# Layer 0 of a two-layer scan network: the partitions onto which three shifted copies for the dilated taps are written

## The chip, the cores and the metric

The kernel runs on one core of a Trainium2 chip. The metric is the device time of one execution in microseconds. Before the change three runs took 26,064.51, 26,128.44 and 26,154.08 us; their median, 26,128.44 us, is the time that the change is compared with.

## The reference, cut to what matters

The input is `x` with shape (4, 128, 128, 192): four images of 128 x 128 points with 192 channels. Two layers follow each other. Layer 0 normalises, projects to 384 channels, runs a 3x3 depthwise convolution, then a scan over all 16,384 points of an image. The scan's result, `h_map`, goes through three depthwise 3x3 convolutions with dilations 1, 3 and 5, which are added. Only this last part is touched by the change:

```python
def _dwconv_replicate(x, w, dil, pad):
    xp = jnp.pad(x, ((0, 0), (0, 0), (pad, pad), (pad, pad)), mode='edge')
    return lax.conv_general_dilated(xp, w, (1, 1), 'VALID', rhs_dilation=(dil, dil),
        dimension_numbers=('NCHW', 'OIHW', 'NCHW'), feature_group_count=x.shape[1])
...
h1 = _dwconv_replicate(h_map, k3, 1, 1)
h2 = _dwconv_replicate(h_map, k3_1, 3, 3)
h3 = _dwconv_replicate(h_map, k3_2, 5, 5)
h_f = alpha[0] * h1 + alpha[1] * h2 + alpha[2] * h3
```

A layer norm over channels, a gate and an output projection follow. Layer 1 is a different network with four scans and isn't touched.

## The kernel before, in words

**Stages.** `transpose_in` brings the input to channel-major form (span 0 to about 480 us). `layer0` follows; its loads of shifted copies are issued from 561.3 to 5,767.7 us. `in_conv`, `scans` and `outputs` do layer 1 in the rest of the span.

**Layer 0.** An image is cut into 16 chunks of 8 image rows (1,024 points), and the 384 channels into 3 blocks of 128 partitions. For each chunk and block, `project_in` (TensorE, L431), `conv_in` (nine products on ScalarE, L488, added by GpSimd, L493) and `scan` (VectorE, L580) produce the scan's result `hp`, padded at the sides to rows of 138 elements, and `store` (L559) writes it to the DRAM scratch `hpad`. One chunk behind, `half` handles 4 image rows (512 points) at a time, and `item` (from L594) does one block of 128 channels of such a half: 4 images x 16 chunks x 2 halves x 3 blocks are 384 items.

**The dilated taps.** For each of the two dilations 5 and 3, an item loads three copies of its rows from `hpad`, shifted by -dilation, 0 and +dilation image rows. The tile `sa` has 96 partitions and 4 groups of 4 x 138 elements. The 128 channels of a block are seen as 4 groups of 32, so the free dimension counts the groups and the partitions hold 32 channels x 3 copies. `load` (L603 to L608) issues three DMAs from the SP queue, one a copy. Each writes 32 partitions, a row of 2,208 bytes for each of 4 groups, 276 KB in all. `mm` (L610 to L619) then runs 12 matmuls: for each of three horizontal offsets and four groups, the weights `diag[:, d, s, k, g]` (96 x 32) hold one tap weight for each channel and copy, so that one matmul sums three vertical taps of 32 channels into 32 partitions of the PSUM bank `o`. There are two dilations, so an item has 6 loads and 24 such matmuls. The eight taps of dilation 1 beside the middle one are done by VectorE (`taps`, L635) from a tile `hh` that is loaded by L624, and the middle tap is folded into `diag`.

**What sets the order.** `Order.emit` plans layer 0 on the host from costs written beside each step and replays the steps in that order on all engines. A load of shifted copies is one planned step with cost 1.5 and size 848e3, a matmul step of 12 costs 2.7, and the planner's DMA rate is 250e3 bytes a microsecond. Each of the tiles `sa0` and `sa1` has two buffers, and the PSUM bank has two. SP takes its DMAs in the planned order; before each it waits for the buffer to be free.

**Set up once.** `mask` (L318 to L320, 96 x 32) has a one where a partition belongs to a channel of the group; `diag` (L322 to L328) is the product of the tap weights `wk` with it. `wk` and `wc` are arranged on the host in `layout`.

Of the kernel before, what the change touches and what calls it, by code (L numbers as in the profile page):

```python
# [12 lines left out]
ALU = mybir.AluOpType  # L13
# [8 lines left out]
HC = C // 2  # L22
NB = 3
PAD = 5
HW_ = W + 2 * PAD
# [175 lines left out]
class Maker:  # L201
# [60 lines left out]
    def layer0(self, xT, x1T, hpad, xsd, gn_in, gnd, gn_out, w, ident, p96, eps):  # L262
# [6 lines left out]
        nc, tc = self.nc, self.tc  # L269
        ctx = ExitStack()  # L270
        with ctx:
# [16 lines left out]
            wk = cp.tile([HC, 2, 3, NB, 4], F32, name="wk")  # L288
            nc.sync.dma_start(wk, w["wk0"])
            wc = cp.tile([HC, 2, NB, 4], F32, name="wc")  # L290
# [10 lines left out]
            def v(k, i):  # L301
                return vec[:, k, i : i + 1]
# [13 lines left out]
                )  # L316
                nc.vector.tensor_tensor(wk[:, 0, 1], wk[:, 0, 1], wc[:, d], ALU.add)
            mask = cp.tile([HC, 32], F32, name="mask")  # L318
            nc.vector.tensor_tensor(mask, ident[:HC, 0:32], ident[:HC, 32:64], ALU.add)
            nc.vector.tensor_tensor(mask, mask, ident[:HC, 64:96], ALU.add)  # L320
            nw = 2 * 3 * NB * 4
            diag = cp.tile([HC, 2, 3, NB, 4, 32], F32, name="diag")  # L322
            nc.vector.tensor_tensor(
# [10 lines left out]
            def buf(tag, bufs, *shape, pool=p1, stream=None):  # L334
                return Buf(pool, tag, bufs, list(shape), stream)
# [258 lines left out]
            def item(b, j, h, k, Cb):  # L594
                r0 = PAD + R * j + 4 * h
                lo, hi = (r0 - 2 * PAD) // R, (r0 + 3) // R
                near = [("h", b, c, k) for c in range(max(lo, 0), min(hi, NCH - 1) + 1)]
                src = hpad[b][k * 128 : k * 128 + 128].rearrange("(g c) x -> c g x", c=32)
                o = buf("hf", 2, 128, 512, pool=psH)
                for d, dil in enumerate(DILS):  # L600
                    t = buf(f"sa{d}", 2, HC, 4, 4 * HW_)

                    def load(t=t, dil=dil):  # L603
                        for a in range(3):
                            c = (r0 + (a - 1) * dil) * HW_
                            nc.sync.dma_start(
                                t()[32 * a : 32 * a + 32], src[:, :, c : c + 4 * HW_]
                            )  # L608

                    def mm(t=t, d=d, dil=dil):  # L610
                        x = t().rearrange("p g (r w) -> p g r w", w=HW_)
                        for s in range(3):
                            c0 = PAD + (s - 1) * dil
                            for g in range(4):
                                nc.tensor.matmul(  # L615
                                    o()[32 * g : 32 * g + 32], diag[:, d, s, k, g],
                                    x[:, g, :, c0 : c0 + W],
                                    start=(d == 0 and s == 0), stop=(d == 1 and s == 2),
                                )  # L619

                    op("SP", 1.5, load, reads=near, writes=[t], size=848e3, early=-192)
                    op("PE", 2.7, mm, reads=[t], writes=[o], early=-456)
                hh, xr = buf("hh", 2, 128, 6, HW_), buf("xsr", 2, 128, 512)
                op("SP", 0.5, lambda: nc.sync.dma_start(  # L624
                    hh().rearrange("p r w -> p (r w)"),
                    hpad[b][k * 128 : k * 128 + 128, (r0 - 1) * HW_ : (r0 + 5) * HW_],
                ), reads=near, writes=[hh], size=424e3)
                c1 = j * T + h * 512
                op("SP", 0.4, lambda: nc.sync.dma_start(
                    xr(), xsd[b][k * 128 : k * 128 + 128, c1 : c1 + 512]  # L630
                ), reads=[("xs", b, j, k)], writes=[xr], size=262e3)
                def taps(which):
                    o3 = o().rearrange("p (r w) -> p r w", w=W)
                    for col, dy, dx in which:
                        nc.vector.scalar_tensor_tensor(  # L635
                            o3, hh()[:, 1 + dy : 5 + dy, PAD + dx : PAD + dx + W],
                            v(k, V0_K + col), o3, ALU.mult, ALU.add,
                        )

                for q in range(0, 8, 2):  # L640
                    op("DVE", 1.57, lambda q=q: taps(NEAR[q : q + 2]), reads=[hh], writes=[o], early=-966)
                y = buf("y", 6, 128, 512)

                def combine():
                    nc.vector.tensor_tensor(o(), o(), Cb(), ALU.mult)
                    nc.vector.scalar_tensor_tensor(  # L646
                        y(), xr(), v(k, V0_DS), o(), ALU.mult, ALU.add
                    )

                op("DVE", 1.45, combine, reads=[Cb, xr], writes=[o, y])  # L650
                return y
# [946 lines left out]
def pair_pack(w):  # L1598

    t = np.zeros((128, 6, 128), np.float32)  # L1600
    t[:, AA] = w[:128, :128]
    t[:64, MA] = w[128:, :128]
    t[64:, MC] = w[128:, :128]
    t[:, AM, :64] = w[:128, 128:]
    t[:, CM, 64:] = w[:128, 128:]
    t[:64, MM, :64] = w[128:, 128:]
    t[64:, MM, 64:] = w[128:, 128:]
    return t


def block_rows(v):

    return np.concatenate([v[:128], v[128:], v[128:]])


def layout(a):
    n = {k: np.asarray(v) for k, v in a.items()}
    l0 = {k[8:]: v for k, v in n.items() if k.startswith("L0_conv_")}
    l1 = {k[8:]: v for k, v in n.items() if k.startswith("L1_conv_")}
    w = {"x": n["x"].reshape(B, L, C)}  # L1620
    w["p96"] = np.kron(np.eye(HC // 6), np.full((6, 6), 1 / 6)).astype(np.float32)

    w["win0"] = l0["Win"].T
    xp = np.zeros((NB * 128, 32), np.float32)
    xp[:, : DR + 2] = l0["x_proj_w"].T
    w["xp0"] = xp
    dtw = np.zeros((2, 32, NB * 128), np.float32)
    dtw[:, :DR] = l0["dt_w"].T
    dtw = dtw.reshape(64, NB * 128)
    w["dtw0"] = dtw  # L1630
    w["wout0"] = l0["Wout"].T
    w["alpha"] = l0["alpha"].reshape(1, 3)
    w["vec0"] = np.concatenate(
        [l0["conv_w"].reshape(-1, 9)]
        + [l0[x].reshape(-1, 1) for x in ("conv_b", "dt_b", "A_logs", "Ds")]
        + [l0["k3"].reshape(-1, 9)]
        + [l0[x].reshape(-1, 1) for x in ("ln_g", "ln_b")],
        axis=1,
    )


    wk = np.stack([l0[x].reshape(NB, 4, 32, 3, 3) for x in ("k3_2", "k3_1")])
    wk = wk.transpose(4, 3, 0, 5, 1, 2).copy()
    wc = np.zeros((3, 32, 2, NB, 4), np.float32)
    for d, x in enumerate(("k3", "k3_1")):
        wc[1, :, d] = l0[x].reshape(NB, 4, 32, 9)[..., 4].transpose(2, 0, 1)
    wk[1, :, 1, 1] = 0
    w["wk0"], w["wc0"] = wk.reshape(HC, 2, 3, NB, 4), wc.reshape(HC, 2, NB, 4)

    w["wx1"] = pair_pack(l1["in_proj_w"][:, :C])  # L1650
    w["wz1"] = pair_pack(l1["in_proj_w"][:, C:])
    xp = np.zeros((128, 4, 3, 128), np.float32)
    dtw = np.zeros((128, 4, 3, 128), np.float32)
    nd = DR + 2 * NS
    for k in range(4):
        pw, dw = l1["x_proj_w"][k], l1["dt_w"][k]
        xp[:, k, 0, :nd] = pw[:128]
        xp[:64, k, 1, :nd] = pw[128:]
        xp[64:, k, 1, 64 : 64 + nd] = pw[128:]
        xp[:, k, 2, 64 : 64 + nd] = pw[:128]  # L1660
        dtw[:DR, k, 0] = dw[:, :128]
        dtw[:DR, k, 1, :64] = dw[:, 128:]
        dtw[64 : 64 + DR, k, 1, 64:] = dw[:, 128:]
        dtw[64 : 64 + DR, k, 2] = dw[:, :128]
    w["xp1"], w["dtw1"] = xp, dtw
    wo = np.zeros((128, 3, C), np.float32)
    wo[:, 0] = l1["out_w"][:128]
    wo[:64, 1] = l1["out_w"][128:]
    wo[64:, 2] = l1["out_w"][128:]
    w["wout1"] = wo  # L1670
    w["vec1"] = block_rows(
        np.concatenate(
            [l1["conv_w"].reshape(C, 9)]
            + [l1[x].reshape(C, 1) for x in ("conv_b", "ln_g", "ln_b")]
            + [l1["dt_b"].T],
            axis=1,
        )
    )

    w["al1"] = l1["A_logs"].reshape(4, 3, 64, 2, NS // 2).transpose(3, 2, 1, 0, 4).reshape(128, -1)  # L1680
    w["ds1"] = np.tile(l1["Ds"].reshape(4, 3, 64).transpose(2, 1, 0), (2, 1, 1))
    return {k: np.ascontiguousarray(v) for k, v in w.items()}
# [23 lines left out]
```

## Time and profile before

| What | From the page or the trace |
|---|---|
| Runs | 26,064.51 to 26,154.08 us, median 26,128.44 us |
| Profiled execution | span 26,077.3 us; what lies around the span isn't listed |
| TensorE busy | 23,595.6 us, 90% of the span |
| VectorE, ScalarE, GpSimd busy | 84%, 80%, 79% |
| DMA moved | 4,171.84 MB, mean 160 GB/s |
| `sa<-hpad` | 2,304 issues, 276 KB each, 8.0 us from issue to landing |
| L615, matmuls on `sa` | 18,432 instructions, 2,191.8 us busy |
| L635, the near taps | 3,072 instructions, 2,316.2 us busy |

The page cuts the span into 40 slices of about 652 us. Layer 0 fills the slices from the first to the ninth. "Busy" is time in which an instruction of the engine was under way; matmuls are pipelined, and their ends are modelled. The DMA digit is the mean busy share of 16 DMA engines.

### The profile page before, as it was taken

The page shows a single profiled execution, that of the slowest core. Times are in us where ns is not written, and L with a number is a line of the kernel's source. Part 1 is how long each engine was busy: PE and PEld are TensorE (multiplying, and loading weights), DVE is VectorE, ACT ScalarE, POOL GpSimd, SP SyncE. Part 2 cuts the span into 40 slices and gives each one's busy share as a digit, 9 for nine tenths or more (in the row PEclk, how much of TensorE's full clock was granted, in tenths as well). Part 3 has the DMA queues.
Part 4 walks back from the last instruction along what each step waited for, and adds up shares of the span by engine and source line. Part 5 has one row for each costly group of instructions (what it writes and reads, how often), then busy time and mean ns, then how long its engine had stood idle before and what let it go on. Part 6 is the DMA issues. An engine that isn't in the chain of part 4 may idle for free.

```text
span 26077.3 us, 435537 instructions
## 1 busy us (share of the span) xinstructions
PE 23595.6 (90%) x168196; PEld 8682.5 (33%) x168196; DVE 21939.2 (84%) x15401; ACT 20827.2 (80%) x24211; POOL 20540.0 (79%) x9962
## 2 busy tenths in 40 slices
PE   4999999998799999999999999999999999999699
PEld 2323232222233333333333333333333333333245
DVE  3889888888788889998988988888998989999643
ACT  5989899966688888888888888888888888888543
POOL 3999899955588888888888888888888888899500
PEclk6999999999899999999999999999999999999899
DMA  6999999985544444444444444444544444455563
GB/s 205 246 246 251 239 249 246 243 219 200 162 127 130 130 129 135 135 127 116 125 117 132 135 132 128 129 130 131 137 134 132 121 119 121 131 139 138 193 232 107
DMA packets 1646421, 4171.84 MB, mean 160 GB/s; under 512 B 236800, under 2 KB 387776, under 8 KB 1641280
## 3 DMA queue, kind: packets, MB, share of 16 engines
q1 hardware_dynamic: 1644352, 4143.97, 58.0%
q8 instruction: 1333, 21.84, 0.4%
q14 instruction: 736, 6.03, 0.1%
HBM read 3203.95 MB, written 939.10 MB: 159 GB/s over the span
## 4 chain that ended last, share of the span: by engine, by line
PE 47%; DVE 21%; ACT 13%; issue 7%; DMA 6%; POOL 5%; SPq 1%; DVEq 0%; POOLq 0%; ACTq 0%
DVE h L1250 14%; PE f L1217 13%; PE Y L1264 10%; ACT h L1228 6%; PE hf L615 5%; ACT dA L1244 3%; PE s L1071 3%; POOL hc L1256 2%; PE s L1094 2%; POOL xs L493 2%; PE g L706 2%; PE f L723 2%; DVE hf L635 2%; PE z L828 1%; DMA C<-cs 1%
## 5 line engine op out<-in xcount | busy, mean ns | idle before, releaser
L1256 POOL TENSOR_TENSOR hc<-h,C 128x1024 f32<-128x1024 f32 x6144 | 14345.2, 2364 | 2265.0 <-PE Y L1264 1087.3
L1250 DVE TENSOR_TENSOR_SCAN h<-dA,st,h 128x1024 f32<-128x1024 f32 x5760 | 13131.7, 2334 | 708.5 <-ACT st L1280 275.2
L1228 ACT COPY h<-f 128x1024 f32<-128x1024 f32 (+3 forms) x8192 | 6343.2, 801 | 2094.0 <-PE f L1217 2028.7
L1217 PE MATMUL f<-D,dT 32*64 32x256 f32 x98304 | 7087.0, 404 | 795.8 <-ACT h L1228 649.7
L1264 PE MATMUL Y<-hc,sel 128*64 128x512 f32 x24576 | 6928.0, 651 | 479.9 <-POOL hc L1256 223.6
L1244 ACT ACTIVATE dA<-d,alog 128x1024 f32<-128x1024 f32 x6144 | 6917.7, 1126 | 313.0 <-DVE h L1250 260.4
L1217 PEld LDWEIGHTS f<-D,dT 32*64 32x64 f32 x98304 | 3253.3, 136 | 6620.9 <-ACT h L1228 4804.6
L493 POOL TENSOR_TENSOR xs<-xs,pr 128x1024 f32<-128x1024 f32 x1536 | 3640.4, 2372 | 251.8 <-ACT pr L488 185.7
L635 DVE SCALAR_TENSOR_TENSOR hf<-hh,vec,hf 128x512 f32<-128x512 f32 x3072 | 2316.2, 754 | 251.4 <-PE hf L615 125.9
L1264 PEld LDWEIGHTS Y<-hc,sel 128*64 128x64 f32 x24576 | 1314.5, 140 | 2959.6 <-issue 1770.9
L615 PE MATMUL hf<-sa,diag 96*32 96x512 f32 x18432 | 2191.8, 614 | 78.5 <-DVE y L646 43.6
L1143 DVE TENSOR_TENSOR D<-s,mask 128x1024 f32<-128x1024 f32 x1024 | 1241.7, 1213 | 842.6 <-PE s L1137 842.6
L488 ACT ACTIVATE pr<-xi,vec 128x1024 f32<-128x1024 f32 x1536 | 1706.7, 1144 | 175.8 <-POOL xs L493 172.8
L615 PEld LDWEIGHTS hf<-sa,diag 96*32 96x32 f32 x18432 | 555.0, 111 | 1616.5 <-issue 1348.7
L1104 POOL TENSOR_TENSOR u<-l,u 128x1024 f32<-128x1024 f32 x384 | 908.2, 2365 | 165.2 <-ACT l L1097 137.1
L1250 DVE TENSOR_TENSOR_SCAN h<-dA,h 128x1024 f32<-128x1024 f32 x384 | 856.8, 2276 | 64.3 <-ACT dA L1244 32.2
L1094 PE MATMUL s<-pj,w 128*128 128x512 f32 x1536 | 894.2, 665 | 7.1 <-ACT l L1097 2.0
L1071 PE MATMUL s<-u,w 128*128 128x512 f32 x1536 | 749.2, 625 | 53.2 <-DMA prev<-xc 52.5
L706 PE MATMUL g<-xz,w 96*128 96x512 f32 x1536 | 769.1, 626 | 28.6 <-DVE y L699 14.8
L1097 ACT ACTIVATE l<-s,vec 128x512 f32<-128x512 f32 x768 | 529.1, 689 | 325.3 <-PE s L1094 320.7
L1137 PEld LDWEIGHTS s<-ident,pj 128*128 128x128 f32 x4096 | 550.0, 195 | 593.0 <-issue 251.6
L939 DVE SCALAR_TENSOR_TENSOR acc<-xi,vec,acc 128x1024 f32<-128x1024 f32 x384 | 715.0, 1862 | 26.8
(209 smaller groups left out, 21241.3 us busy)
## 6 DMA issues: line engine op xcount, KB each, us to landing
C<-cs SPq DMA_DIRECT2D x4096, 256.0 KB, 4.8
sa<-hpad SPq DMA_DIRECT2D x2304, 276.0 KB, 8.0
d<-delta SPq DMA_DIRECT2D x1536, 256.0 KB, 4.1
u<-xc SPq DMA_DIRECT2D x384, 512.0 KB, 4.7
delta<-l SPq DMA_DIRECT2D x384, 512.0 KB, 3.7
y<-y SPq DMA_DIRECT2D x1536, 128.0 KB, 3.3
hh<-hpad SPq DMA_DIRECT2D x384, 414.0 KB, 8.0
hpad<-hp SPq DMA_DIRECT2D x192, 552.0 KB, 8.3
```

Of the source, the lines that this page charges most:

```text
L488: op("ACT", 1.1, lambda pr=pr, t=t: nc.scalar.activation(rows(pr()), x()[:, t // 3 : t // 3 + R, t % 3 : t % 3 + W], AF.Copy, scale=v(k, V ...
L493: op("POOL", 2.38, lambda pr=pr: nc.gpsimd.tensor_tensor(o(), o(), pr(), ALU.add), reads=[pr], writes=[o], early=-390)
L615: nc.tensor.matmul(o()[32 * g : 32 * g + 32], diag[:, d, s, k, g], x[:, g, :, c0 : c0 + W], start=(d == 0 and s == 0), stop=(d == 1 and s ...
L635: nc.vector.scalar_tensor_tensor(o3, hh()[:, 1 + dy : 5 + dy, PAD + dx : PAD + dx + W], v(k, V0_K + col), o3, ALU.mult, ALU.add,)
L1071: nc.tensor.matmul(g(), wt()[:, 0, i], uu[i]()[:, 512 * c : 512 * c + 512], start=(i == 0), stop=(i == 2),)
L1094: op("PE", 0.9, lambda g=g, c=c: nc.tensor.matmul(g(), wt()[:, 1, i], x()[:, 512 * c : 512 * c + 512], start=True, stop=True,), reads=[wt, ...
L1217: nc.tensor.matmul(gs()[64 * jn : 64 * jn + 64, n, 256 * a : 256 * a + 256], td()[rt, r // 64, 2 * sb + a], tD()[rt, a, 256 * jn : 256 * j ...
L1228: nc.scalar.copy(H[:, at : at + nq, 256 * sb : 256 * sb + 256].rearrange("p q (a r s) -> p q a r s", a=2, s=32)[:, :, :, 2 * rp : 2 * rp + 2],
L1244: op("ACT", 1.16, lambda: nc.scalar.activation(a(), d(), AF.Exp, scale=alog[:, c : c + 1]), reads=[d], writes=[a], table="exp", early=-522)
L1250: nc.vector.tensor_tensor_scan(hs[:, way], a()[:, way], hs[:, way], 0.0 if at == 0 else s0()[:, q : q + 1], ALU.mult, ALU.add,)
L1256: op("POOL", 2.4, lambda: nc.gpsimd.tensor_tensor(t(), hs, tC(), ALU.mult), reads=[hq, tC], writes=[t])
L1264: nc.tensor.matmul(ym()[64 * th : 64 * th + 64], sel, t()[:, 512 * th : 512 * th + 512], start=(q == 0), stop=(q == NQ - 1),)
```

## The change

The partition of a channel `c` and a copy `a` in the tile `sa` becomes `3*c + a`; it was `32*a + c`. So a load writes every third of the 96 partitions, where it wrote 32 that lie side by side. Bytes, number of DMAs, number of matmuls and their shapes stay. The mask, and the tap weights that the host lays out, are rearranged to match: on the device one reduction takes the place of two additions, once in the kernel.

```diff
             mask = cp.tile([HC, 32], F32, name="mask")
-            nc.vector.tensor_tensor(mask, ident[:HC, 0:32], ident[:HC, 32:64], ALU.add)
-            nc.vector.tensor_tensor(mask, mask, ident[:HC, 64:96], ALU.add)
+            nc.vector.tensor_reduce(
+                mask, ident[:HC, :HC].rearrange("p (c a) -> p c a", a=3),
+                mybir.AxisListType.X, ALU.add,
+            )
...
                         for a in range(3):
                             c = (r0 + (a - 1) * dil) * HW_
-                            nc.sync.dma_start(
-                                t()[32 * a : 32 * a + 32], src[:, :, c : c + 4 * HW_]
-                            )
+                            nc.sync.dma_start(t()[a:HC:3], src[:, :, c : c + 4 * HW_])
...
-    wk = wk.transpose(4, 3, 0, 5, 1, 2).copy()
-    wc = np.zeros((3, 32, 2, NB, 4), np.float32)
+    wk = wk.transpose(3, 4, 0, 5, 1, 2).copy()
+    wc = np.zeros((32, 3, 2, NB, 4), np.float32)
     for d, x in enumerate(("k3", "k3_1")):
-        wc[1, :, d] = l0[x].reshape(NB, 4, 32, 9)[..., 4].transpose(2, 0, 1)
-    wk[1, :, 1, 1] = 0
+        wc[:, 1, d] = l0[x].reshape(NB, 4, 32, 9)[..., 4].transpose(2, 0, 1)
+    wk[:, 1, 1, 1] = 0
```

## The prediction

> **What bounds the kernel now.** The change touches layer 0 alone, so I asked first for the busy times before, in and after the stretch in which shifted copies are loaded and used (window view; the numbers after each stretch are its length and then busy us of TensorE, weight loads, VectorE, ScalarE, GpSimd, the granted clock, the DMA share and GB/s):
>
> ```profile
> core 0: us, PE busy (x) PEld busy (x) DVE busy (x) ACT busy (x) POOL busy (x), PEclk, DMA share, GB/s
> 0.00:560.00 560.00, 236.96 (x1218) 172.33 (x1218) 188.13 (x311) 254.40 (x269) 148.19 (x97) 0.69 0.65 203
> 560.00:5790.00 5230.00, 5056.38 (x26065) 1551.19 (x26064) 4576.00 (x5897) 4621.13 (x5120) 4642.89 (x2940) 0.97 0.96 244
> 5790.00:26077.00 20287.00, 18302.26 (x140918) 6959.00 (x140916) 17175.07 (x9194) 15951.67 (x18823) 15748.94 (x6927) 0.94 0.49 137
> ```
>
> In these 5,230 us two resources are nearly full: DMA at 0.96 and TensorE at 5,056 us (97%, with modelled ends). VectorE, ScalarE and GpSimd stand at 87 to 89%. Later the DMA share is 0.49, so nothing there can gain from cheaper transfers.
>
> Is the DMA slow because of these very loads? I looked for neighbouring stretches with and without them (DMA view of two 10 us stretches: the rate, then what was issued):
>
> ```profile
> DMA packets 1371, 3.35 MB, mean 335 GB/s; under 512 B 170, under 2 KB 362, under 8 KB 1369
> ...
> q1 hardware_dynamic: 1369, 3.32, 100.9%
> ```
>
> ```profile
> DMA packets 1120, 2.20 MB, mean 220 GB/s; under 512 B 124, under 2 KB 124, under 8 KB 1120
> ...
> q1 hardware_dynamic: 1120, 2.20, 105.2%
> ...
> sa<-hpad SPq DMA_DIRECT2D x6, 276.0 KB, 6.1
> ```
>
> The first is 4,550 to 4,560 us, when other transfers are moving; the second is 4,560 to 4,570, when all data packets are the 2,208-byte rows of `sa`. The engines are full in both, yet the rate is 335 against 220 GB/s. So a byte of `sa` costs half as much again as another. The packet records say the same: over layer 0 a 2,208-byte packet takes 166 ns in the median and 89 ns in the quickest tenth, two humps a factor of two apart, while packets of 2,048 bytes from other loads have a median of 89 ns.
>
> Does anyone wait for it? The waits of SP and the engines, and the chain that ended last (line, us in total, times, longest):
>
> ```profile
> SPq L606 <- PE hf L615: 699.2, 392, 8.8
> SPq L624 <- DVE hf L635: 520.0, 214, 12.3
> SPq L606 <- DMA sa<-hpad: 354.6, 439, 2.5
> ```
>
> ```profile
> 1803.06 9.72 DMA sa<-hpad
> ...
> 1812.86 9.86 DMA hpad<-hp
> ...
> 1822.73 10.46 DMA sa<-hpad
> ...
> 1833.28 11.77 DMA hpad<-hp
> ```
>
> SP waits mostly for engines to free the double buffers, so DMA isn't the pacer everywhere; but there are stretches such as 1,790 to 1,876 us in which the chain is nothing but transfers of 10 us each. Adding all pieces that the chain names DMA between 560 and 5,790 us gives 370 us (`sa` 197, `hpad` stores 55, `hh` 52, `xsr` 33, the rest 33). TensorE holds 2,858 us of the same chain. Engines' idle time that ended directly with a landing is smaller, some 110 us over all engines together.
>
> [...]
>
> **The change part by part.**
>
> *Mask and weights.* Two VectorE additions of 124 and 186 ns become one reduction of the same 96 x 96 input, once, at 383 us. Taken as zero; even 1 us would be nothing. Rearranged weights change neither count nor shape of the 18,432 matmuls at L615 (2,192 us busy). All 96 rows of `sa` and of the weights are read in both forms, only in another order, so a gain or a loss has no source that the trace shows: zero.
>
> *Issue.* 2,304 DMAs on SP, a median of 383 ns each in the row of L606. The access pattern has the same dimensions with another partition step, and the row of issues shows no stride to price it. Bounds: 0 to +0.5 us an issue. SP waits over 350 us behind its own earlier loads and over 1,200 us for buffers, so +0.1 us (230 us) lies in waits. [...] I take zero.
>
> *The transfers.* [...] From 0.96 x 5,230 = 5,020 us it falls to 4,280, a share of 0.82 at unchanged length.
>
> *What of it reaches the end.* The 740 us don't, because TensorE has 5,056 busy us in the same stretch: it lacks 174 us of being full, plus whatever stalls hide under modelled ends. What shortens is the 370 us of DMA on the chain. A landing takes 8.0 us in the median now. At layer 1's lower DMA share a 256 KB load lands in 4.7 us, and the six loads above, alone on the queue, in 6.1; with less crowding I take 5.5. 370 x (1 - 5.5/8.0) = 115 us. [...] Upper end: all landings fall to the shortest on record, 3.2 us: 222 us. Next late is then TensorE at L615 with the PSUM bank that VectorE frees at L646, and GpSimd's additions at L493.
>
> Sum against the profiled execution: 26,077 - 115 = 25,962 us. The median of the runs is 51 us above the span, so 26,128 - 115 = 26,013, rounded to 26,010. What this kernel's measurement can tell from no change is about 0.3%, 78 us.
>
> **The rivals.**
>
> *Hidden anyway.* SP's 699 us of waiting for TensorE say that the loads run ahead as far as two buffers let them. The direct idle time by landings is only 110 us, spread over four engines, and where a wait is removed the engine next to it may be late by as much. Then 15 to 78 us come through: 26,080 us.
>
> *DMA was the pacer.* At a share of 0.96 every wait may be a late transfer in disguise, such as VectorE waiting 126 us for the matmuls at L615. Then the stretch falls to TensorE's floor or a little below its modelled one: 174 to 300 us less, 25,880 us. Against it: the chain gives DMA only 7%.
>
> [...]
>
> *It doesn't do what it says.* [...] packets stay at 160 ns and the time at 26,130 us. The quickest tenth at 89 ns speaks against it.
>
> **How the numbers follow.** Chances: forecast (78 to 180 us gained) 0.46; DMA the pacer 0.10; hidden 0.33; no effect 0.05[...]. Faster by over 0.3% is 0.46 + 0.10 = 0.56, same 0.33 + 0.05 = 0.38, slower 0.06. The range reaches from the pacer's 25,880 to 26,135, which takes in hidden and no effect; what it leaves out is the crowding and a pacer's gain beyond 250 us.
>
> **What would show it.** Right: the DMA share between 560 us and the end of layer 0 falls to 0.78 to 0.86; 2,208-byte packets fall from 160 to 105 to 130 ns in the mean; `sa<-hpad` lands in 5 to 6.5 us; the chain's DMA part falls below 260 us; L615's busy time stays within 1%; layer 1 stays at about 20,290 us. Wrong: packets unchanged[...], issue at L606 above 0.5 us, or a landing that falls to 5.5 us with a stretch that still takes over 5,180 us (hidden), or below 5,040 us (pacer).

## The result and the profile after

The changed kernel took 26,104.29 us in the median of 12 runs, the kernel before 26,123.15 us in 12. The ratio is 0.9993 with a 95% interval of 0.9974 to 1.0012: no difference that this measurement can tell. Forecast were 26,010 us and a change clear of 0.3%.

The window view of the changed kernel, with the same stretches as before (busy us of TensorE, weight loads, VectorE, ScalarE, GpSimd, then clock, DMA share and GB/s):

```profile
560.00:5790.00 5230.00, 5045.75 (x26098) 1553.47 (x26096) 4590.12 (x5934) 4629.45 (x5136) 4648.77 (x2947) 0.98 0.89 245
5790.00:26077.00 20287.00, 18340.32 (x140620) 6948.08 (x140620) 17147.42 (x9150) 15909.41 (x18796) 15743.47 (x6921) 0.94 0.49 137
```

The DMA share fell from 0.96 to 0.89, at the same rate: the engines are busy for less time with the same bytes. The tile view of `sa` before (matmuls and issues with their ns min/median/max and the first and last start; landing):

```profile
L615 PE MATMUL hf<-sa,diag x18432: 590/592/1063, 569.6 to 5779.9; 96*32 96x512 f32 x199
L606 SPq DMA_DIRECT2D sa<-hpad x2304: 302/383/2327, 561.3 to 5767.7; - x192
...
DMA to landing us min/median/max: 3.2/8.0/13.5
```

The same view of the changed kernel, then who SP waited for:

```profile
L615 PE MATMUL hf<-sa,diag x18432: 590/592/1063, 570.5 to 5736.8; 96*32 96x512 f32 x199
L608 SPq DMA_DIRECT2D sa<-hpad x2304: 554/592/1957, 562.6 to 5724.1; - x192
...
DMA to landing us min/median/max: 3.3/6.2/12.8
```

```profile
SPq L608 <- PE hf L615: 747.4, 443, 8.7
SPq L624 <- DVE hf L635: 570.4, 246, 12.3
...
SPq L608 <- DMA sa<-hpad: 131.5, 219, 1.2
```

A load lands in 6.2 us where it took 8.0, and SP waits 131 us for earlier loads where it waited 355. An issue takes 592 ns where it took 383. Added up over all of SP's lines from 560 to 5,790 us, its waits for landings fell from 1,262 to 484 us, its waits for engines grew from 2,249 to 2,509 us, and the issues of copies took 475 us more: part of what was gained went into waiting for buffers that are freed no sooner, and most of the rest into the longer issue. A stretch of 10 us at 3,300 us, in which 1,133 of 1,273 packets are rows of `sa`, shows the new rate with the engines full (DMA view):

```profile
DMA packets 1273, 2.53 MB, mean 253 GB/s; under 512 B 132, under 2 KB 132, under 8 KB 1272
...
q1 hardware_dynamic: 1272, 2.52, 102.1%
```

That is 253 against the 220 GB/s of the prediction's stretch. In the packet records the mean of a 2,208-byte packet went from 160 to 142 ns, and DMA work (the sum of all packet times over 16 engines, 560 to 5,790 us) from 5,046 to 4,668 us.

Where did the time go? In the two profiled executions the last matmul on a shifted copy starts at 5,779.9 us before and at 5,736.8 us after, 43 us earlier. What follows took 20,297 us before and 20,386 us after, 88 us more, although the change touches nothing there. The granted clock is the share of TensorE's full clock that it was given, averaged over time. The 12 runs of the changed kernel spread from 25,978 us at a mean granted clock of 0.946 to 26,215 us at 0.935, in step with the clock. So a layer 0 that is shorter by some 40 us can't be seen in a run of the whole kernel. The experiments therefore time layer 0 by itself.

### The profile page after: what moved, and what is told of

The parts are those of the page before. It is cut to its first block, busy times and chain, and to the rows that moved or that the text cites. A ratio compares the mean times of both kernels' runs of the same rounds, so it can differ in the third digit from the quotient of the medians.

```text
span 26122.3 us, 435536 instructions
## 1 busy us (share of the span) xinstructions
PE 23658.7 (91%) x168196; PEld 8704.1 (33%) x168196; DVE 21934.3 (84%) x15400; ACT 20802.7 (80%) x24211; POOL 20539.1 (79%) x9962
## 4 chain that ended last, share of the span: by engine, by line
PE 43%; DVE 19%; ACT 12%; issue 6%; DMA 4%; POOL 4%; SPq 1%; DVEq 0%; POOLq 0%; ACTq 0%
DVE h L1250 14%; PE f L1217 13%; PE Y L1264 10%; ACT h L1228 6%; ACT dA L1244 3%; PE s L1071 3%; PE hf L615 3%; POOL hc L1256 2%; PE s L1094 2%; PE z L828 1%; DMA C<-cs 1%; DVE D L1143 1%; DVE acc L939 1%; PE f L723 1%; PE g L706 1%
## 5 line engine op out<-in xcount | busy, mean ns | idle before, releaser
L615 PE MATMUL hf<-sa,diag 96*32 96x512 f32 x18432 | 2173.9, 610 | 78.8 <-DVE y L646 40.3
L615 PEld LDWEIGHTS hf<-sa,diag 96*32 96x32 f32 x18432 | 553.4, 110 | 1599.4 <-issue 1340.0
L706 PE MATMUL g<-xz,w 96*128 96x512 f32 x1536 | 764.2, 622 | 26.6 <-DVE y L715 14.0
```

The costliest lines, as they stand in the source:

```text
L615: nc.tensor.matmul(o()[32 * g : 32 * g + 32], diag[:, d, s, k, g], x[:, g, :, c0 : c0 + W], start=(d == 0 and s == 0), stop=(d == 1 and s ...
```

## Experiments

### Layer 0 alone, its ceiling, and the stride alone

Four kernels on one chip end after layer 0; layer 1 is left out, and one corner of the scratch is written as output.

```diff
     mk.layer0(xT, x1T, hpad, xsd, gn0, gn0d, gn1, w, ident, p96, eps)
-    xc = [
...
-    mk.outputs(y, x1T, gn1, out, wz, wout, vec, ident, eps)
+    for b in range(B):
+        nc.sync.dma_start(out[b, 0:C, :], x1T[b][:, 0:C])
```

Layer 0 before: 

> Layer 0 of the kernel before alone; layer 1 is left out and a corner of the scratch is written as output. Every theory: 5,780 to 5,880 us, the DMA share in the stretch of the loads at 0.96. It is the base for the other runs of this group, and its spread tells how much of the whole kernel's spread comes from layer 1: if layer 1 makes it, the five runs lie within 0.3% of each other.

Layer 0 changed: 

> Layer 0 of the changed kernel alone, layer 1 left out. Theory 'covered' (engines other than DMA set layer 0's length, what the transfers gain shows only where a landing was late): 25 to 60 us less than layer 0 before, as the last matmul on the copies came 43 us earlier in the profiles. Rival 'nothing' (the 43 us are chance): within 15 us. Rival 'issue eats it' (the longer issue on SP takes back most of the gain): also 25 to 60 us, it is told apart by the run with strides and unchanged ports.

A quarter of the copies' bytes (each load brings one of four channel groups, and all matmuls read that one):

```diff
-                                t()[32 * a : 32 * a + 32], src[:, :, c : c + 4 * HW_]
+                                t()[32 * a : 32 * a + 32, 0], src[:, 0, c : c + 4 * HW_]
...
-                                    x[:, g, :, c0 : c0 + W],
+                                    x[:, 0, :, c0 : c0 + W],
```

> Layer 0 before, layer 1 left out; each load of a shifted copy brings one of its four channel groups, and all matmuls read that group, so the number of loads and matmuls stays and the bytes of these loads fall to a quarter. DMA work falls by about 2,200 us of 5,050. Theory 'covered': 50 to 130 us less than layer 0 before, since TensorE stays at 5,050 busy us. Rival 'too small a relief' (the DMA does pace layer 0, and the change only gave back half of what was reckoned): over 200 us less.

Strided, but with two of the copies kept inside partitions 0 to 63 and the third at 64 to 95:

```diff
-                                t()[32 * a : 32 * a + 32], src[:, :, c : c + 4 * HW_]
+                                t()[(a if a < 2 else 64) : (a + 63 if a < 2 else HC) : (2 if a < 2 else 1)], src[:, :, c : c + 4 * HW_]
```

> Layer 0 before, layer 1 left out; the copies -dilation and 0 are written to the even and the odd partitions of 0 to 63 (step 2), the third stays at 64 to 95[...], but two of three loads are strided. The tap weights keep their places, so the taps of these two copies are mixed up. Issue of a strided load near 590 ns, of the third near 380. Theory 'covered': within 25 us of layer 0 before. Rival 'issue eats it': 40 us or more slower, as SP gets 320 us more to do.

| Layer 0 alone | Median us | Runs from to | Against before |
|---|---|---|---|
| before | 5,819.9 | 5,812.1 to 5,834.4 | |
| changed | 5,782.7 | 5,780.7 to 5,786.1 | -37 |
| a quarter of the bytes | 5,776.8 | 5,768.4 to 5,783.3 | -43 |
| strided, copies in 0 to 63 and 64 to 95 | 5,815.8 | 5,808.0 to 5,842.3 | -4 |

The gain is real, 37 us or 0.6% of layer 0: the runs don't overlap. Those of before spread by 0.4%, so layer 1 makes only a part of the whole kernel's spread. It is also nearly all that cheaper copies can give: with a quarter of their bytes only 6 us more come, short of the 50 to 130 us that I expected. The stretch from 560 to 5,640 us of the three kernels before, changed and quarter, in this order (window view):

```profile
560.00:5640.00 5080.00, 4909.96 (x25296) 1508.01 (x25296) 4439.66 (x5708) 4573.33 (x5068) 4617.33 (x2921) 0.97 0.97 245
```

```profile
560.00:5640.00 5080.00, 4920.14 (x25557) 1512.40 (x25556) 4477.84 (x5766) 4587.51 (x5085) 4625.98 (x2929) 0.98 0.90 248
```

```profile
560.00:5640.00 5080.00, 4918.37 (x25569) 1513.91 (x25568) 4483.23 (x5772) 4588.38 (x5088) 4622.09 (x2930) 0.98 0.52 154
```

The DMA share goes from 0.97 to 0.90 to 0.52, and TensorE gets through 25,296, 25,557 and 25,569 matmuls: the first step of relief gives 261 more, the second, five times as large, gives 12. The row of L615 shows how little of TensorE's standing was ended by a landing (group view of before and of quarter; busy us and mean ns, then TensorE's idle time ahead and what ended it):

```profile
L615 PE MATMUL hf<-sa,diag 96*32 96x512 f32 x17808 | 2111.2, 612 | 77.0 <-DVE y L646 41.9 <-issue 15.6 <-DMA sa<-hpad 15.4
```

```profile
L615 PE MATMUL hf<-sa,diag 96*32 96x512 f32 x18024 | 2111.6, 606 | 69.1 <-DVE y L646 40.4 <-issue 18.3 <-DMA sa<-hpad 5.9
```

Of 77 us in which TensorE stood before these matmuls, 15.4 were ended by a landing, and 41.9 by VectorE at L646, which frees the PSUM bank. A quarter of the bytes takes the first down to 5.9 and leaves the second.

That is less than the 37 and 43 us gained. Most of the gain stands elsewhere, in TensorE's busy time (pages of before, changed and quarter):

```profile
PE 5304.9 (91%) x27312; PEld 1732.5 (30%) x27312; DVE 4780.2 (82%) x6237; ACT 4879.8 (84%) x5401; POOL 4792.4 (82%) x3038
```

```profile
PE 5268.2 (91%) x27312; PEld 1721.3 (30%) x27312; DVE 4776.9 (83%) x6236; ACT 4879.3 (84%) x5401; POOL 4792.2 (83%) x3038
```

```profile
PE 5261.1 (91%) x27312; PEld 1722.6 (30%) x27312; DVE 4778.0 (83%) x6237; ACT 4878.4 (84%) x5401; POOL 4786.7 (83%) x3038
```

With the same 27,312 matmuls TensorE is busy for 37 and 44 us less. The profiled spans shrank by 46 and 50 us, so its idle time shrank by only 9 and 6. The granted clock rose with it: 0.943 to 0.946 in the runs of before, 0.949 to 0.950 in those of changed, 0.950 to 0.953 in those of the quarter. After 560 us the clock records of the three traces have TensorE at half its clock for 302, 227 and 217 us. So on this chip, as far as busy times with modelled ends can tell, most of the gain shows as TensorE running faster, not as TensorE waiting less. Whether shorter waits keep the clock up, or something else moves both, no run here parts.

The fourth kernel settles two things. Two of three loads are strided there, and the median issue is 583 ns; but the mean 2,208-byte packet stays at 160 ns and the time is within its spread of before. So the stride alone, here a step of 2, doesn't make transfers faster; a step of 3 over all 96 partitions brought 142 ns in the changed kernel. And the longer issue, 415 us more work for SP (1,346 against 932 us for all copies), costs nothing that shows. The rival that issue eats the gain falls.

### The loads by themselves

One kernel with no computing issues loads in six groups, one after the other, into 8 tiles in turn. The loads of the first five groups differ in the partitions they write, and groups 3 and 4 take two copies to a tile:

```diff
+        for a in range(3):
+            nc.sync.dma_start(t[32 * a : 32 * a + 32], ...)
...
+            nc.sync.dma_start(t[a:HC:3], ...)
...
+            nc.sync.dma_start(t[64 * a : 64 * a + 32], ...)
...
+            nc.sync.dma_start(t[a:128:4], ...)
```

> Loads alone, no computing, six groups one after the other, each load 276 KB of 2,208-byte rows taken from the input unless said: (1) three copies at partitions 0, 32 and 64; (2) three copies with step 3; (3) all at 0 and 32; (4) at 0 and 64 in turn; (5) step 4 over 128 partitions; (6) 128 partitions of 8,832 bytes, 1,104 KB. [...] Rival 'it is the compute beside it that holds (2) at 252': (2) reaches 285 or more here.

| Group | Partitions | GB/s | Mean packet, ns |
|---|---|---|---|
| 1 | 0, 32 and 64 upwards | 224 | 165 |
| 2 | step 3 of 96 | 255 | 146 |
| 3 | 0 and 32 upwards | 202 | 184 |
| 4 | 0 and 64 upwards | 245 | 152 |
| 5 | step 4 of 128 | 387 | 95 |
| 6 | 128, rows of 8,832 bytes | 421 | 334 |

The kernel ran once. Rates are bytes by the time from a group's first to last packet. Group 1 runs near the 220 GB/s of the prediction's stretch, group 3 below it. The page of this kernel shows the steps in its slices:

```profile
DMA  9999999999999999999999999999999999999998
GB/s 209 224 224 224 224 226 226 225 229 255 256 257 259 259 254 248 230 204 203 203 203 203 203 237 245 245 246 246 282 396 394 392 395 408 426 427 425 427 426 350
```

The engines are full throughout, at rates from 203 to 427 GB/s: here a full DMA share says nothing on the rate. Group 2 runs at 255 GB/s as in the kernel, so no computing beside it holds it there, and the rival falls. Step 3 wins only 14% over group 1. Two copies in turn at 0 and 64 (group 4, 245 GB/s) are 21% faster than at 0 and 32 (group 3, 202), and group 1, with copies at all three places, lies between at 224. Whether transfers to partitions that lie far apart overlap, or why else they are quicker, no group shows. A step of 4 over 128 partitions gives 387 GB/s and 95 ns a packet.

### Without the cover: fewer matmuls

Three kernels on one chip run 8 of the 24 matmuls of an item (the middle horizontal offset); layer 1 is left out.

```diff
-                        for s in range(3):
+                        for s in (1,):
...
-                                    start=(d == 0 and s == 0), stop=(d == 1 and s == 2),
+                                    start=(d == 0), stop=(d == 1),
```

Before: 

> Layer 0 before, layer 1 left out, and of the 24 matmuls on shifted copies of an item only the 8 of the middle horizontal offset are run, so TensorE loses some 1,400 us of 5,050 and the loads stay as they are. Theory 'TensorE covers the transfers': DMA, with 5,050 us of work, is next, so layer 0 shortens by 50 to 150 us against 5,820. Rival 'the chain of VectorE, ScalarE and GpSimd covers them': under 40 us.

Changed: 

> Layer 0 of the changed kernel with the same 8 of 24 matmuls, layer 1 left out. Theory 'TensorE covers the transfers': without that cover the change is worth much more than 37 us: 100 to 350 us less than the run with few matmuls and the placement of before (DMA work differs by 384 us). Rival 'the other engines cover them': 20 to 60 us less.

A quarter of the bytes: 

> Layer 0 before with 8 of 24 matmuls and a quarter of the bytes of the shifted copies, layer 1 left out: the floor that VectorE, ScalarE and GpSimd set in this order of steps. Theory 'TensorE covers the transfers': 5,400 to 5,600 us. Rival 'the other engines cover them': 5,700 to 5,780, within 30 us of the run with few matmuls and the changed placement.

Measured: 5,887.3, 5,876.5 and 5,855.2 us. All are longer than the full layer 0 on the other chip, 5,819.9 us, which no theory foresaw, and they lie only 11 and 32 us below the first. The chip isn't the reason: the whole kernel before took 26,104 us on it and 26,143 on the other. All three miss the ranges of the theory that TensorE covers the transfers; the 11 us and the 5,855 miss those of the rival too. The window view and the row of L706 of the first show what changed:

```profile
560.00:5640.00 5080.00, 4305.18 (x13316) 1288.25 (x13314) 4389.87 (x5645) 4534.20 (x5041) 4585.73 (x2908) 0.82 0.95 243
```

```profile
L706 PE MATMUL g<-xz,w 96*128 96x512 f32 x1452 | 971.9, 806 | 203.1 <-DVE y L699 131.5 <-DVE y L715 70.9
```

TensorE has half its matmuls, and its granted clock falls from 0.97 to 0.82; the gate projection at L706, which isn't touched, takes 806 ns each where it took 624. So the remaining matmuls got slower while others were taken away, and as a test of TensorE as the cover this is inconclusive; why the clock fell no run shows. But TensorE now isn't busy for 775 of 5,080 us, 202 of them ahead of L706 until VectorE's steps at L699 and L715 end, and layer 0 is no shorter: the sum of TensorE's work alone isn't what sets the length here. It does show that with 16 matmuls an item gone DMA still isn't next: freed of three quarters of the `sa` bytes, layer 0 gains 32 us.

### Without the cover: less on the three other engines

Two kernels, with 4 of 8 near taps and 5 of 9 taps of the first convolution left out, and layer 1 left out.

```diff
-                for q in range(0, 8, 2):
+                for q in range(0, 4, 2):
...
-                for t in range(9):
+                for t in range(5):
```

Before: 

> Layer 0 before, layer 1 left out, with 4 of 8 near taps and 5 of 9 taps of the first convolution: VectorE loses some 1,160 us, GpSimd 1,820, ScalarE 880; TensorE and the loads keep all their work. Theory 'TensorE sets the length': 5,700 to 5,820 us, at most 120 less than the full layer 0. Rival 'VectorE, GpSimd and ScalarE set it in the fixed order of steps': they gone, DMA and TensorE with 5,050 us each are left, 5,640 to 5,690 us.

Changed: 

> Layer 0 of the changed kernel with the same work left out on VectorE, GpSimd and ScalarE, layer 1 left out. Theory 'TensorE sets the length': 20 to 60 us less than the light run with the placement of before, as in the full layer 0. Rival 'VectorE, GpSimd and ScalarE cover the transfers': 80 us less or more, since DMA work differs by 384 us and only TensorE is left beside it.

Measured: 5,692.8 and 5,678.1 us, 127 and 105 us less than the full layer 0 in each placement. Some 30 us of the 127 are gained ahead of the first load, which is issued at 530.9 us instead of 560.0. The two placements differ by 15 us, against 37 in the full layer. The window view of both:

```profile
560.00:5640.00 5080.00, 4958.55 (x25892) 1534.14 (x25888) 3428.94 (x4346) 3879.27 (x4388) 2858.73 (x2163) 0.98 0.99 250
```

```profile
560.00:5640.00 5080.00, 4969.88 (x25942) 1537.11 (x25934) 3439.38 (x4362) 3879.47 (x4391) 2860.91 (x2165) 0.98 0.92 250
```

VectorE, ScalarE and GpSimd are at 68, 76 and 56%, and layer 0 isn't much shorter. TensorE still takes nearly the whole stretch: relieving three engines of 15 to 38% of their work gives 2% of layer 0. The length decides nothing: 5,692.8 us lies 7 below what the theory of TensorE expected (5,700 to 5,820) and 3 above what the rival expected (5,640 to 5,690). The 15 us between the placements lie 5 below the first theory's range, but the rival that the three engines cover the transfers wanted 80 or more; it falls. In this pair the clock is the same, 0.956, and TensorE's idle time before L615 that ended with a landing fell from 20.8 to 9.8 us, which is most of the 15. What is left fits TensorE as the floor, or a chain in which its steps and those of the other engines alternate. The runs don't part the two: the one that took TensorE's work away lost the clock. Of the 127 us here, 52 are again TensorE busy for less time with the same matmuls, at a clock of 0.956 against 0.945.

### A step of 4 over 128 partitions, and a puzzle

The tile takes 128 partitions, four for a channel; the fourth copy is zeroed once and has zero weights. Two fixed tiles for each dilation keep the zeros.

```diff
-                    t = buf(f"sa{d}", 2, HC, 4, 4 * HW_)
+                    t = buf(f"sa{d}", 2, 128, 4, 4 * HW_)
+                    t.tile = sa[d][made[d] % 2]
+                    made[d] += 1
...
-                            nc.sync.dma_start(t()[a:HC:3], src[:, :, c : c + 4 * HW_])
+                            nc.sync.dma_start(t()[a:128:4], src[:, :, c : c + 4 * HW_])
```

Layer 0 alone: 

> Layer 0 of the changed kernel, layer 1 left out, with the tile of the copies over 128 partitions, four a channel, the fourth zeroed once and given zero weights: a load writes every fourth of 128 partitions[...]. Alone such loads ran at 387 GB/s where step 3 ran at 255. Theory 'the transfers are covered': 5,770 to 5,790 us, within 12 us of step 3, as a quarter of the bytes gave 5,777. Rival 'more relief, more gain': 5,750 us or less.

The whole kernel: 

> The whole kernel with a step of 4 over 128 partitions. Theory 'covered, and layer 1 hides the rest in its spread': 0.9965 to 1.0005 of the kernel before, with an interval of 0.002 either way, so no gain can be told although layer 0 is some 43 us shorter. Rival 'more relief, more gain': ratio 0.996 or less.

Layer 0 took 5,761.4 us on the chip where before had taken 5,819.9: 58 us less, more than the quarter of the bytes gave, so the expectation of 5,770 to 5,790 missed, and so did the rival's of 5,750 or less. The whole kernel has a ratio of 1.0004 (0.9987 to 1.0022). To part the transfer from the wider tile, four kernels ran together on another chip; the new one has the wider tile and the copies at 0, 32 and 64:

```diff
-                            nc.sync.dma_start(t()[a:128:4], src[:, :, c : c + 4 * HW_])
+                            nc.sync.dma_start(t()[32 * a : 32 * a + 32], src[:, :, c : c + 4 * HW_])
```

Before: 

> Layer 0 before, layer 1 left out, as the base on this chip. Both theories: 5,800 to 5,835 us. If it is 5,800 or less, the chip is part of the 58 us.

Changed: 

> Layer 0 of the changed kernel, layer 1 left out: 30 to 45 us less than the base of this group by both theories.

Step of 4: 

> Layer 0, layer 1 left out, step of 4 over 128 partitions. Theory 'the chip': within 10 us of step 3 on the same chip. Theories 'relief' and 'wider tile': 15 to 30 us less than step 3.

Wider tile alone: 

> Layer 0, layer 1 left out, a tile of 128 partitions with copies at 0, 32 and 64 as before, the last 32 partitions zeroed once and given zero weights: matmuls of 128 rows, transfers as before. Theory 'wider tile': 15 to 30 us less than the base, with a higher granted clock. Theory 'relief': within 10 us of the base.

| Layer 0, median us | Copies side by side | Spread by a step |
|---|---|---|
| 96 partitions | 5,811.4 | step 3: 5,780.1 |
| 128 partitions | 5,791.5 | step 4: 5,761.8 |

Across: the spread is worth 31 us with 96 partitions and 30 us with 128, although step 3 wins 14% in rate and step 4 some 70%. Down: the wider tile is worth 20 and 18 us whichever way the copies lie. The two effects add. Each is measured on four or five runs; the two kernels with copies side by side overlap by 1 us (5,787 to 5,800 and 5,799 to 5,815), the other neighbours in the table lie apart. The window view of step 3 and step 4 shows the relief that brought nothing more:

```profile
560.00:5640.00 5080.00, 4923.49 (x25561) 1514.38 (x25558) 4479.98 (x5769) 4588.17 (x5085) 4624.85 (x2926) 0.98 0.90 248
```

```profile
560.00:5640.00 5080.00, 4914.71 (x25654) 1514.39 (x25652) 4496.76 (x5789) 4597.34 (x5096) 4635.23 (x2933) 0.99 0.78 249
```

The 20 us of the wider tile come with a higher granted clock (over the whole span 0.948 before, 0.953 with the wider tile) and 35 us less busy time of TensorE. That matmuls of 128 rows keep the clock up isn't shown; another form of buffer goes with it. Step 3 gains differently on this chip: of the 32 us between the profiled spans, 16 are TensorE's busy time and 16 its idle time, and the clocks of the runs overlap (0.947 to 0.950 and 0.948 to 0.951).

## Why the prediction was wrong, point by point

**The bound.** Right that DMA and TensorE are both nearly full in layer 0 and that `sa` is the slow part. Wrong in what a full DMA share was worth. The engines were at work on loads that SP had issued as far ahead as the buffers allowed; it waited 2,249 us for engines to free them. With a quarter of the copies' bytes the share is 0.52 and layer 0 is 0.7% shorter.

**The transfers.** Right that they get faster when the copies are spread, and not by the stride alone: with a step of 2 inside 64 partitions a packet took 160 ns, with a step of 3 over 96 it took 142. The size was off: the fall of DMA work from 5,020 to 4,280 us was my estimate, which no trace from before the change shows. By the rates of the loads alone a copy takes 1.26 us at 224 GB/s and 1.11 at 255. DMA work fell by 377 us, not 740, so the share came to 0.89 and the packets to 142 ns, short of the signs named; the landing, at 6.2 us, was within its range. This term didn't decide the result: a step of 4 cuts DMA work by 1,060 us and gains no more.

**Issue.** Taken as zero with 0 to +0.5 us as bounds; it is +0.21 us, 475 us of SP's time in all, and it lay in waits as argued.

**What reaches the end: the step that failed.** "What shortens is the 370 us of DMA on the chain", and by "370 x (1 - 5.5/8.0) = 115 us". The landing fell to 6.2, and by that formula 83 us should have come. Layer 0 gained 37 and 31 us. Even with landings at 2.2 us, where the formula gives 268, it gained 43. The 370 us were the length of transfers on one path, not the delay that they cause: when they shorten, another path ends nearly as late. The chain shows that. In the changed kernel's layer 0 alone it can be followed back to 3,110 us. From there to the last matmul on a copy it names DMA for 44 us, where before it named DMA for 192; but it names TensorE for 1,791 us, where before it named TensorE for 1,688. So 149 us of transfers left the chain, 103 us of TensorE's work came in, and the stretch is 45 us shorter. The prediction read TensorE's part of the chain as 2,858 us; it was 2,959.

A smaller number stood beside the 370 us and was used for a rival: the engines' idle time that ended with a landing, recorded as 110 us over four engines (they add up to 97), and 15 us ahead of L615. The rival "hidden anyway" built on it, and its range, 15 to 78 us, holds the 37 and 31. That is in part luck. Ahead of L615 the landings' part fell by only 3 us in the changed kernel and by 10 in the quarter, while TensorE's busy time fell by 37 and 44: neither the forecast nor the rival had a term for the clock.

**The measurement.** The forecast needed 78 us to be told from no change. 37 us of 26,100 are 0.14%, and layer 1 alone moved by 88 us between two profiled executions.

**The other rivals.** DMA as pacer: out, since a quarter of the bytes gives 43 us. Crowding, which would have made transfers slower: packets shrank, from 160 to 142 ns. No effect: layer 0 did shorten.

## What to carry to other kernels

Don't price the relief of a transfer by the length of transfers on the chain; the chain shows one path and not how close the next one is. The idle time that landings end on the busiest engine is a better start, but not a price either: here it was 15 us where 37 came, with a clock that moved along, and 21 where 15 came in the runs with less on the three other engines, where the clock stayed. Cutting the bytes of the suspect in a kernel of the stage alone gave the ceiling in one run, and it could have been had before the change was built. And a full DMA share beside a queue that waits for buffers was no bottleneck here: 0.97 went to 0.52 and layer 0 was 43 us shorter.

## What was not expected

A load that steps over partitions takes 592 ns to issue on SP where one with 32 neighbours takes 383. Loads in turn at partitions 0 and 64 ran at 245 GB/s, those at 0 and 32 at 202. Taking two thirds of the matmuls of one line away lengthened the stage by 1.2% (5,887 us on another chip than the 5,820), as the granted clock fell from 0.97 to 0.82. A tile with 32 zero partitions added to the matmul made layer 0 20 us shorter. Cheaper loads made TensorE's own busy time 37 us shorter on one chip and 16 on another, with the same matmuls.
